# Last part of a two-layer perceiver kernel: attention two tiles ahead of the layers, the first softmax beside the values' products, rounded levels turned before the rounding number is taken off

## The chip, the core and the metric

The kernel runs on one core of one Trainium2 chip. The metric is the device time of one execution in microseconds, here the median of three runs. Engines are named as the profile names them: PE (TensorE, matrix products), PEld (its weight loads), DVE (VectorE), ACT (ScalarE), POOL (GpSimd), SP (SyncE, which issues the DMAs here). PE writes to PSUM, which has eight banks of 512 f32 numbers per partition; the kernel deals them out to pools of two or three buffers.

## The reference, cut to what matters

The whole is six blocks on `x` of 8 batches x 64 queries x 512 numbers (float32), each added to `x`. The first four (a cross attention over 1601 context rows, a spectral block, a routed feed-forward block, a second cross attention) are the same in both kernels. The change touches the last two and the seam before them:

```python
def _L1_attn_ref(x, Wq, Wk, Wv, u, v, Wo, bo):
    # 16 heads of 32
    Q, K, V = heads(x @ Wq), heads(x @ Wk), heads(x @ Wv)
    r = _sinusoid_rel_pos(S, dk)
    term1 = jnp.einsum('bhqd,bhkd->bhqk', Q, K)
    term2 = jnp.einsum('bhqd,kd->bhqk', Q, r)
    term3 = jnp.einsum('hd,bhkd->bhk', u, K)[:, :, None, :]
    term4 = jnp.einsum('hd,kd->hk', v, r)[None, :, None, :]
    scores = (term1 + term3 + _rel_shift(term2 + term4)) / jnp.sqrt(dk)
    attn = jax.nn.softmax(scores, axis=-1)
    out = jnp.einsum('bhqk,bhkd->bqhd', attn, V).reshape(B, S, H * dv)
    return out @ Wo + bo

def _L1_ffn_ref(x, w1, b1, w2, b2):
    def act_quant(x):
        scale = 127.0 / jnp.clip(jnp.max(jnp.abs(x), axis=-1, keepdims=True), 1e-05)
        q = jnp.clip(jnp.round(x * scale), -128.0, 127.0) / scale
        return x + jax.lax.stop_gradient(q - x)
    def bitlinear(x, w, b):
        xq = act_quant(rmsnorm(x))
        wq = weight_quant(w)          # -1, 0 or 1 times one scale
        return jnp.einsum('bsd,fd->bsf', xq, wq) + b
    h = bitlinear(x, w1, b1)          # 512 -> 2048
    h = jax.nn.gelu(h, approximate=False)
    return bitlinear(h, w2, b2)       # 2048 -> 512

x = x + _L1_attn_ref(_layernorm(x, axis=-1), ...)
x = x + _L1_ffn_ref(_layernorm(x, axis=-1), ...)
```

## The kernel before, in words

The 512 query rows are four tiles of 128 rows (two batches of 64 each), kept in SBUF as `x[:, t, :]` throughout. `l1_xattn` is the second cross attention. It goes over eight batches; each makes scores of four head groups against 1601 keys, a softmax, the values' products, and for the batch after it the keys. After batches 2, 4 and 6 begin, `project_out` adds the result to tiles 0, 1 and 2 of `x`; tile 3 is added at the very end. So in the last batch tiles 0 to 2 of `x` are already what the last part reads.

`l1_tail` is the last part: self attention with relative positions, then the two layers. Its steps, by name and line:

- `Group.turn` (L1698 on): normalises a tile (`K.normalizer`, L63; statistics on DVE L81 and L82, the power on POOL L56, the normalised tile `xn` L68), turns it on PE (`xt_ps`, L1702) and copies it on ACT (`xT`, L1703). There is one `xn` buffer. The first group holds tiles 0 to 2, the last group tile 3 alone.
- `Group.queries` (L1712 on): the queries' product (`q_ps`, L1707), from which DVE makes `qu` (L1717) for the scores and ACT makes `qv` (L1725) for the positions. Both read the same PSUM bank, in the order of the code.
- `positions_of` (L1749 on): products of `qv` with the position table (`y_ps`, L1740), copied by DVE and ACT (L49, L51) to `y`, two buffers; four DMAs per tile write `y` to DRAM (`shift`, L1757). `shifted` (L1772 on): four DMAs per tile read it back skewed by one (`z`, L1776), which is the reference's `_rel_shift`.
- `keys_and_values` (L1793 on): keys for a group (`k_ps`, L1707, copied at L1798), then values tile by tile (`v_ps`, L1802).
- `probabilities` (L1808 on): scores (`s_ps`, also L1740, 16 products), `z` added (L1815), then the softmax: maximum L1819, subtraction L1820, exp on ACT L1821, sum L1822, reciprocal L1823, product L1824.
- `turn` (L1827 on), `attend` (L1838 on), `out` (L1861 on): transposes of the probabilities (`pT_ps`, L1833; copies L1834), their product with the values (`o_ps`, L1846), masking to own heads (`oT`, L1855 on ACT and L1856 on DVE), the output product (`out_ps`, L1864) and its addition to `x` (L1871).
- `hidden` (L1873 on): statistics of `x`, normalisation, levels (`rms_levels`, L1614 on), turning (`xT_ps`, L1888, copied at L1889), the first layer in four pieces of 512 (`h_ps`, L1896), scaled by DVE (L1900), GELU (L1901) and squares (L1903) on ACT, maxima on DVE (L1904).
- `hidden_levels` (L1907 on): the levels of all 2048 numbers. `layer2` (L1918 on): turning (`hT_ps`, L1923; copies by `K.copy`, DVE and ACT in turn), the second layer (`o2_ps`, L1927, shown as `o_ps`), scaling with the bias `b2` (L1929), addition of `x` (L1930) and the output DMA (L1931).

`rms_levels` rounds by adding and subtracting 1.5 x 2^23 (`MAGIC`). It makes two passes over its data: one scales in place (L1629), one rounds into a bf16 copy (L1630: `xq`, 512 wide, and `hq`, 2 x 1024).

The order at the end of `l1_tail` is written out by hand:

```python
keys_and_values(first)
p = {0: probabilities(0)}
last.turn(); last.queries(); positions_of(FIRST, last.qv[0])
out(0, attend(0, turn(p[0])))
p[1] = probabilities(1)
keys_and_values(last); shifted(FIRST)
for t in range(NT):
    h = hidden(t)
    if got: layer2(t - 1, *got)
    if t + 1 < NT: out(t + 1, attend(t + 1, turn(p[t + 1])))
    got = hidden_levels(*h)
    if t + 2 < NT: p[t + 2] = probabilities(t + 2)
layer2(NT - 1, *got)
```

(cut, with calls drawn together). This order is not each engine's order word for word. The framework lays out every engine's queue ahead of the run; of what it holds ready it takes what stands first in the code. In the trace PE does some of the last part's L1702 between the cross attention's L1461, and its L1707 keys between L1740 positions. At run time each queue is worked off in its order.

PSUM in the last part: pool `e` three banks (`xt_ps`, `q_ps`, `y_ps`, `h_ps`), pool `mm` three banks (`k_ps`, `v_ps`, `s_ps` two at a time, `pT_ps`, `o_ps` two at a time, `out_ps`, `o2_ps`), pool `t` two (`xT_ps`, `hT_ps`).

Of the kernel before, what the change touches and what calls it, by code (L numbers as in the profile page):

```python
# [10 lines left out]
F32 = mybir.dt.float32  # L11
# [8 lines left out]
P = 128  # L20
# [12 lines left out]
class Ctx:  # L33
# [29 lines left out]
    def normalizer(self, pool, x):  # L63

        _, mv, rstd = self.statistics(pool, x)

        def norm(t, out):
            self.nc.vector.tensor_scalar(  # L68
                out, x[:, t, :], mv[:, t, 0:1], rstd[:, t : t + 1], ALU.subtract, ALU.mult
            )  # L70

        return norm
# [1147 lines left out]
def l1_xattn(K, x, d):  # L1220
# [7 lines left out]
    with ExitStack() as es:  # L1228
# [257 lines left out]
        for b in range(B):  # L1486
# [16 lines left out]

            s[0] = scores(b, 0, r_of[0])
# [47 lines left out]
class TernaryWeights:  # L1552
# [5 lines left out]
    def __init__(self, K, pool, memory, d):  # L1558
        nc = self.nc = K.nc
        self.ident = pool.tile([P, P], BF16, tag="identq", name="identq")  # L1560
        nc.vector.tensor_copy(self.ident, K.ident)
# [52 lines left out]
def rms_levels(K, pool, y, top, mean_square, out):  # L1614
# [10 lines left out]
    nc.vector.tensor_scalar_mul(scale, scale, 127.0)  # L1625
    nc.vector.tensor_scalar_mul(level, top, 1.0 / 127.0)
    n = min(y.shape[-1], 1024)
    for i in range(y.shape[-1] // n):
        nc.vector.tensor_scalar(y[:, ts(i, n)], y[:, ts(i, n)], rms, scale, ALU.mult, ALU.mult)  # L1629
        nc.vector.tensor_scalar(out[:, ts(i, n)], y[:, ts(i, n)], MAGIC, MAGIC, ALU.add, ALU.subtract)  # L1630
# [3 lines left out]
def l1_tail(K, x, d, w):  # L1634
# [8 lines left out]
    with ExitStack() as es:  # L1643
        ep = es.enter_context(tc.tile_pool(name="e_e", bufs=1))
        sp = es.enter_context(tc.tile_pool(name="e_n", bufs=3))
# [41 lines left out]
        class Group:  # L1687
# [8 lines left out]
            def turn(self):  # L1696
                for i, t in enumerate(self.tiles):
                    xn = ep.tile([P, D], F32, tag="xn", name="xn")  # L1698
                    K.normalizer(sp, x[:, t : t + 1, :])(0, xn)
# [11 lines left out]
            def queries(self):  # L1711
                self.qv = [ring("q", "qv") for _ in self.tiles]  # L1712
                for c in range(DC):
                    ps = bank("q_ps")[:, : len(self.tiles) * P]
                    self.project(wq, c, ps)
                    for s in range(2):
                        nc.vector.tensor_scalar(  # L1717
                            self.qu[:, c, :, :, s, :].rearrange("p n b q -> p (n b) q"),
                            ps.rearrange("p (b q) -> p b q", q=S),
                            uv[:, 0, c : c + 1], own[:, s : s + 1], ALU.add, ALU.mult,  # L1720
                        )
                    for i in range(len(self.tiles)):
                        q = ps[:, ts(i, P)].rearrange("p (b q) -> p b q", b=2)
                        for s in range(2):
# [3 lines left out]
                            )  # L1728

# [63 lines left out]
        def keys_and_values(g):  # L1793
            n = len(g.tiles) * P
            for c in range(DC):
                ps = pm.tile([P, D], F32, tag="mm", name="k_ps")[:, :n]
                g.project(wk, c, ps)
                nc.scalar.copy(kT[:, c, ds(g.tiles[0] * P, n)], ps)  # L1798
            for i, t in enumerate(g.tiles):
# [72 lines left out]

        def hidden(t):  # L1873
# [8 lines left out]
            xq = rp.tile([P, D], BF16, tag="xq", name="xq")  # L1882
            level = rms_levels(K, rp, y, top, square, xq)
            nc.vector.tensor_mul(level, level, w.size[:, 0:1])
            xT = rp.tile([P, DC, P], BF16, tag="xT", name="xT")
            ps = pt.tile([P, 4, P], BF16, tag="t", name="xT_ps")
            for c in range(DC):
                nc.tensor.transpose(ps[:, c, :], xq[:, ts(c, P)], w.ident)  # L1888
            nc.scalar.copy(xT, ps)  # L1889
# [3 lines left out]
            for n in range(4):  # L1893
# [10 lines left out]
                nc.vector.tensor_reduce(tops[:, n : n + 1], hn, AX.X, ALU.max, apply_absolute_value=True)  # L1904
            return h, tops, squares

        def hidden_levels(h, tops, squares):  # L1907
# [5 lines left out]
            hq = rp.tile([P, HID], BF16, tag="hq", name="hq")  # L1913
            level = rms_levels(K, rp, h, top, square, hq)
            nc.vector.tensor_mul(level, level, w.size[:, 1:2])
            return hq, level

        def layer2(t, hq, level):  # L1918
            hT = rp.tile([P, 16, P], BF16, tag="hT", name="hT")
            for n in range(4):  # L1920
                ps = pt.tile([P, 4, P], BF16, tag="t", name="hT_ps")
                for i in range(4):
                    nc.tensor.transpose(ps[:, i, :], hq[:, ts(4 * n + i, P)], w.ident)  # L1923
                K.copy(hT[:, ts(n, 4), :], ps)
# [4 lines left out]
            nc.vector.scalar_tensor_tensor(o, ps, level, b2, ALU.mult, ALU.add)  # L1929
            nc.vector.tensor_add(o, o, x[:, t, :])  # L1930
            nc.sync.dma_start(d["out"][ts(t, P), :], o)  # L1931

        keys_and_values(first)
        p = {0: probabilities(0)}
# [5 lines left out]
        out(0, attend(0, turn(p[0])))  # L1940
        p[1] = probabilities(1)
# [128 lines left out]
```

## Time and profile before

| | us |
|---|---|
| median of 3 runs (lowest to highest) | 3293.55 (3289.65 to 3298.74) |
| the profiled execution, whole | 3301.78 |
| the profiled execution, span from first to last instruction | 3300.0 |
| in it: last batch's softmaxes and `xt_ps`, up to the first `q_ps` | 3061 to 3100.5 |
| queries and positions up to the keys' end | 3100.5 to 3141.9 |
| values, first softmax, first output, to `x` of tile 0 | 3141.9 to 3179.4 |
| four layers and three more attentions | 3179.4 to 3300.0 |

Busy time of PE, DVE, ACT and POOL and the mean granted clock of PE in the four rounds of the layers (from `xT_ps` to the next tile's `xT_ps`; the last to the end):

| us | length | PE | DVE | ACT | POOL | clock |
|---|---|---|---|---|---|---|
| 3189.9 to 3213.9 | 24.0 | 12.98 | 18.12 | 10.54 | 1.65 | 0.86 |
| 3213.9 to 3245.1 | 31.2 | 19.42 | 22.80 | 11.84 | 1.65 | 0.83 |
| 3245.1 to 3272.6 | 27.5 | 17.25 | 19.35 | 9.50 | 1.65 | 0.87 |
| 3272.6 to 3300.0 | 27.4 | 17.40 | 13.45 | 7.80 | 0.55 | 0.81 |

A line of a timeline reads: start, length, engine, source line, operation, output<-inputs, shape, xcount, and in brackets the idle time of the engine just before it and what ended that. A line of the chain of waits reads: start, length, engine, what is made, source line, count. A matmul of f32 numbers is two instructions on PE, and counts as two.

### The profile page before, as it was taken

What the parts mean: (1) busy time and instruction counts of PE and PEld (TensorE: products, weight loads), DVE (VectorE), ACT (ScalarE), POOL (GpSimd) and SP (SyncE); (2) the same over time, 40 slices, a digit from 0 to 9 for tenths busy, and PEclk for the clock granted to TensorE, in tenths of its full rate; (3) what the DMA queues carried; (4) which work ended last, traced back from release to release, by engine and by line L of the source; (5) the groups of instructions that cost most, each with busy time, mean ns of one, the idle gap of its engine ahead of it and who ended that gap; (6) DMA issues with size and microseconds to landing.
All of it is one profiled execution on the core that took longest, in us unless ns stands there. A gap on an engine that the chain in (4) does not pass through costs nothing.

```text
span 3300.0 us, 40525 instructions
## 1 busy us (share of the span) xinstructions
PE 3177.1 (96%) x15881; PEld 2158.4 (65%) x15881; DVE 1761.2 (53%) x2946; ACT 845.9 (26%) x1572; POOL 1006.0 (30%) x976
## 2 busy tenths in 40 slices
PE   8999999999999999998899998999999999999976
PEld 6777778888878888885445444556555565555643
DVE  4755556666566656654333235554546445464656
ACT  3232322222233212211012221323233232222233
POOL 5433344443545544420000044224031231312000
PEclk9999999999999999998899999999999999999888
DMA  7255553333455343226288530010100001000330
GB/s 235 75 168 148 173 174 89 96 98 110 122 171 160 103 134 99 88 87 217 84 308 290 185 108 20 22 40 1 41 20 22 31 11 40 11 21 1 100 74 13
DMA packets 314322, 329.03 MB, mean 100 GB/s; under 512 B 35525, under 2 KB 235717, under 8 KB 312981
## 3 DMA queue, kind: packets, MB, share of 16 engines
q1 hardware_dynamic: 310416, 314.88, 30.4%
q10 hardware_dynamic: 3717, 11.57, 0.9%
q8 instruction: 126, 2.06, 0.3%
q14 instruction: 63, 0.52, 0.0%
HBM read 303.30 MB, written 23.10 MB: 99 GB/s over the span
## 4 chain that ended last, share of the span: by engine, by line
PE 89%; DVE 5%; DMA 3%; ACT 1%; issue 1%; POOL 1%; SPq 0%; ACTq 0%; POOLq 0%; DVEq 0%
PE k_ps L1298 11%; PE v_ps L1397 11%; PE x_ps L566 10%; PE x_ps L451 9%; PE z_ps L566 5%; PE s_ps L1411 4%; PE z_ps L451 4%; PE h_ps L1118 3%; PE oe_ps L1145 3%; PE acc L1461 3%; PE y_ps L566 2%; PE y_ps L451 2%; PE sum_ps L1320 2%; PE s_ps L444 1%; PE v_ps L599 1%; PE qk_ps L237 1%
## 5 line engine op out<-in xcount | busy, mean ns | idle before, releaser
L1335 POOL TENSOR_TENSOR r<-r,minus_half 128x24 f32<-128x24 f32 x64 | 288.8, 4516 | 747.3 <-DVE r L1331 747.3
L1397 PE MATMUL v_ps<-L1x_WvT,ctxT 128*128 128x512 f32 (+1 forms) x832 | 379.7, 604 | 0.0
L1298 PE MATMUL k_ps<-ctxT,L1x_WkT 128*128 128x384 f32 (+1 forms) x1024 | 375.0, 509 | 0.6 <-ACT o L51 0.6
L451 PE MATMUL x_ps<-qt,ctxT 128*128 128x256 f32 x1152 | 287.2, 383 | 7.6 <-DVE s L416 6.0
L566 PE MATMUL x_ps<-pt,ctx 128*128 128x256 f32 x1152 | 280.3, 381 | 1.4 <-ACT u L514 0.9
L1298 PEld LDWEIGHTS k_ps<-ctxT,L1x_WkT 128*128 128x128 f32 x1024 | 184.0, 189 | 140.2 <-issue 42.8
L1397 PEld LDWEIGHTS v_ps<-L1x_WvT,ctxT 128*128 128x128 f32 (+1 forms) x832 | 149.6, 187 | 170.9 <-issue 164.8
L451 PEld LDWEIGHTS x_ps<-qt,ctxT 128*128 128x128 f32 x1152 | 217.4, 191 | 49.2 <-DVE s L416 10.1
L566 PEld LDWEIGHTS x_ps<-pt,ctx 128*128 128x128 f32 x1152 | 216.5, 189 | 35.1 <-DVE a L541 1.6
L122 POOL TENSOR_TENSOR ctxT<-ctxT 128x256 f32<-128x256 f32 x96 | 79.7, 831 | 402.6 <-DMA ctxT<-in_ctxT 355.2
L1411 PEld LDWEIGHTS s_ps<-qb,kT 64*128 64x128 f32 x1664 | 143.8, 187 | 74.8 <-DVE s L1423 44.1
L432 DVE TENSOR_TENSOR m<-m,s 128x512 f32<-128x512 f32 x176 | 134.5, 764 | 94.2 <-ACT s L430 91.6
L122 POOL TENSOR_TENSOR ctx<-ctx 128x256 f32<-128x256 f32 x96 | 72.4, 754 | 344.6 <-DMA ctx<-in_ctx 279.3
L1411 PE MATMUL s_ps<-qb,kT 64*128 64x128 f32 x1664 | 170.9, 287 | 6.7 <-DVE s L1423 6.3
L1302 ACT ACTIVATE kT<-k_ps,L1x_bk 128x384 f32<-128x384 f32 (+1 forms) x128 | 76.1, 594 | 348.9 <-PE k_ps L1298 343.6
L1331 DVE TENSOR_SCALAR r<-sumT_ps 128x12 f32<-128x12 f32 (+1 forms) x128 | 16.5, 166 | 254.5 <-PE sumT_ps L1328 254.1
L1400 ACT COPY v<-v_ps 128x512 f32<-128x512 f32 (+1 forms) x104 | 60.7, 583 | 335.1 <-PE v_ps L1397 335.1
L1423 DVE TENSOR_TENSOR s<-s_ps,r 128x512 f32<-128x512 f32 x192 | 124.7, 683 | 33.3 <-PE s_ps L1411 33.1
L484 DVE TENSOR_TENSOR s<-s,top_ps 128x1024 f32<-128x1024 f32 (+1 forms) x112 | 123.3, 1137 | 21.3 <-PE top_ps L474 21.3
L1452 DVE TENSOR_TENSOR s<-s,top_ps 128x1664 f32<-128x1664 f32 x64 | 117.9, 1884 | 30.0 <-PE top_ps L1448 30.0
L1431 DVE TENSOR_TENSOR fold<-s 128x1536 f32<-128x1536 f32 x64 | 112.1, 1752 | 37.3 <-ACT s L1453 37.3
L416 DVE SCALAR_TENSOR_TENSOR s<-y_ps,bias,p 128x256 f32<-128x256 f32 x96 | 46.3, 483 | 142.9 <-PE y_ps L451 138.4
(408 smaller groups left out, 5777.6 us busy)
## 6 DMA issues: line engine op xcount, KB each, us to landing
w<-in_L0f_W SPq DMA_DIRECT2D x64, 1024.0 KB, 5.5
ctxT<-in_ctxT SPq DMA_DIRECT2D x192, 256.0 KB, 4.5
ctx<-in_ctx SPq DMA_DIRECT2D x192, 256.0 KB, 3.2
ctxT<-in_ctxT SPq DMA_DIRECT2D x24, 768.0 KB, 4.4
wvT<-in_L0x_WvT SPq DMA_DIRECT2D x16, 1024.0 KB, 6.9
qk<-qk_all SPq DMA_DIRECT2D x15, 1024.0 KB, 6.9
qk_all<-stage SPq DMA_DIRECT2D x32, 384.0 KB, 3.4
wraw<-in_L1f_w1T SPq DMA_DIRECT2D x16, 512.0 KB, 4.2
```

The lines of the kernel that those rows point to most:

```text
L122: nc.gpsimd.tensor_add(q[:, 4, :], q[:, 2, :], q[:, 3, :])
L432: nc.vector.tensor_max(self.m, self.m if k else self.s[:, LAST, :], self.s[:, k, :])
L451: nc.tensor.matmul(ps, lhsT=ctxT[i][:, Quarters.LEFT[n], ts(e, P)], rhs=right[n][:, e, :], start=start and e == 0, stop=e == 1, skip_group ...
L484: nc.vector.tensor_sub(s[:, k : k + n], s[:, k : k + n], top.unsqueeze(1).to_broadcast([P, n, HALF]))
L566: nc.tensor.matmul(ps, lhsT=ctx[pair][:, Quarters.LEFT[n], ts(m, P)], rhs=right[n][:, i, :], start=start and i == 0, stop=i == 2, skip_gro ...
L1298: nc.tensor.matmul(ps[:, :n], lhsT=wk[:, e, ts(c, P)], rhs=ctxT[i][:, e, :n], start=e == 0, stop=e == DC - 1)
L1335: nc.gpsimd.tensor_tensor(r[:, at : at + n, :], r[:, at : at + n, :], minus_half[:, :n, :], ALU.pow)
L1397: nc.tensor.matmul(ps[:kn], lhsT=ctxT[i][:, c, ds(at, kn)], rhs=wv[:, c, :], start=c == 0, stop=c == DC - 1)
L1411: nc.tensor.matmul(pair[j][:, i, :], lhsT=kT[c][rows, ts(k0 + i, P)], rhs=qb[rows, c, b].rearrange("p h q -> p (h q)"), start=True, stop=True,
L1423: nc.vector.tensor_mul(out, in_, by)
L1431: nc.vector.tensor_tensor(t, s[:, :, 0:6, :], s[:, :, 6:12, :], op)
L1452: nc.vector.tensor_sub(s[:, j], s[:, j], ps[:, j, :].unsqueeze(1).to_broadcast([P, NK, P]))
```

## The change

It does five things.

1. The statistics of tiles 0 to 2 are made in a pool of their own before the last batch's scores in `l1_xattn` (a callback `in_last`), and handed to the first group's normaliser as `known`.
2. In `queries`, ACT's `qv` stands ahead of DVE's `qu`.
3. `keys_and_values` is two functions. The order is now: first group's keys, probabilities of tile 0, first group's values, output of tile 0, probabilities of tile 1, the last group's turning, queries and positions, output of tile 1, the last group's keys and values. In the loop over the layers, the probabilities and the output are those of tile t + 2.
4. `rms_levels` makes one pass: scale and `MAGIC` added, in place, in f32. The turning on PE is of these f32 numbers (with the f32 identity; the bf16 one is gone), and `MAGIC` comes off in the copy out of PSUM (`turn_levels`): on ACT for `xT`, on DVE and ACT in turn for the four pieces of `hT`. The buffers `xq` and `hq` are gone.
5. `b2` is added to `x` on POOL at the end of `hidden`, and `layer2`'s two DVE operations become one.

```diff
-    def normalizer(self, pool, x):
-        _, mv, rstd = self.statistics(pool, x)
+    def normalizer(self, pool, x, known=None):
+        _, mv, rstd = known or self.statistics(pool, x)
...
+            if not more:
+                in_last()
             s[0] = scores(b, 0, r_of[0])
...
-def rms_levels(K, pool, y, top, mean_square, out):
+def rms_levels(K, pool, y, top, mean_square):
...
     nc.vector.reciprocal(scale, top)
-    nc.vector.tensor_scalar_mul(scale, scale, 127.0)
-    nc.vector.tensor_scalar_mul(level, top, 1.0 / 127.0)
+    nc.vector.tensor_scalar(scale, scale, 127.0, rms, ALU.mult, ALU.mult)
     n = min(y.shape[-1], 1024)
     for i in range(y.shape[-1] // n):
-        nc.vector.tensor_scalar(y[:, ts(i, n)], y[:, ts(i, n)], rms, scale, ALU.mult, ALU.mult)
-        nc.vector.tensor_scalar(out[:, ts(i, n)], y[:, ts(i, n)], MAGIC, MAGIC, ALU.add, ALU.subtract)
+        nc.vector.tensor_scalar(y[:, ts(i, n)], y[:, ts(i, n)], scale, MAGIC, ALU.mult, ALU.add)
+    nc.vector.tensor_scalar_mul(level, top, 1.0 / 127.0)
     return level
...
-                    K.normalizer(sp, x[:, t : t + 1, :])(0, xn)
+                    K.normalizer(rp, x[:, t : t + 1, :], known[t] if t < FIRST else None)(0, xn)
...
+        def turn_levels(y, out, by_vector):
+            ps = pt.tile([P, 4, P], F32, tag="t", name="levels_ps")
+            for i in range(4):
+                nc.tensor.transpose(ps[:, i, :], y[:, ts(i, P)], K.ident)
+            if by_vector:
+                nc.vector.tensor_scalar_add(out, ps, -MAGIC)
+            else:
+                nc.scalar.activation(out, ps, AF.Identity, bias=w.down, scale=1.0)
...
+            nc.gpsimd.tensor_add(x[:, t, :], x[:, t, :], b2)
             return h, tops, squares
...
             for n in range(4):
-                ps = pt.tile([P, 4, P], BF16, tag="t", name="hT_ps")
-                for i in range(4):
-                    nc.tensor.transpose(ps[:, i, :], hq[:, ts(4 * n + i, P)], w.ident)
-                K.copy(hT[:, ts(n, 4), :], ps)
+                turn_levels(h[:, ts(n, 512)], hT[:, ts(n, 4), :], n % 2 == 0)
...
-            nc.vector.scalar_tensor_tensor(o, ps, level, b2, ALU.mult, ALU.add)
-            nc.vector.tensor_add(o, o, x[:, t, :])
+            nc.vector.scalar_tensor_tensor(o, ps, level, x[:, t, :], ALU.mult, ALU.add)
             nc.sync.dma_start(d["out"][ts(t, P), :], o)
...
-        keys_and_values(first)
-        p = {0: probabilities(0)}
+        keys(first)
+        p = probabilities(0)
+        values(first)
+        out(0, attend(0, turn(p)))
+        p = probabilities(1)
         last = Group(wp, [FIRST])
         last.turn()
         last.queries()
         positions_of(FIRST, last.qv[0])
         groups.append(last)
-        out(0, attend(0, turn(p[0])))
-        p[1] = probabilities(1)
-        keys_and_values(last)
+        out(1, attend(1, turn(p)))
+        keys(last)
+        values(last)
         shifted(FIRST)
         got = None
         for t in range(NT):
             h = hidden(t)
             if got:
                 layer2(t - 1, *got)
-            if t + 1 < NT:
-                out(t + 1, attend(t + 1, turn(p[t + 1])))
+            if t + 2 < NT:
+                p = probabilities(t + 2)
             got = hidden_levels(*h)
             if t + 2 < NT:
-                p[t + 2] = probabilities(t + 2)
+                out(t + 2, attend(t + 2, turn(p)))
         layer2(NT - 1, *got)
...
+        known = []
+        with tc.tile_pool(name="early", bufs=NT - 1) as sp:
+            l1_xattn(K, x, d, lambda: known.extend(K.statistics(sp, x[:, t : t + 1, :]) for t in range(NT - 1)))
+            l1_tail(K, x, d, w, known)
```

## The prediction

> **What bounds the kernel now.** The page first: PE is busy for 96% of the span, but the granted clock and PE's digits fall off in the last slices, and the whole change lies there, from about 3061 us on. So the next view is the chain of waits. Its last lines (start, length, engine, what, line):
>
> ```profile
> 3173.31 5.27 PE out_ps L1864 x8
> 3191.02 3.64 PE h_ps L1896 x16
> 3199.29 5.40 PE out_ps L1864 x8
> 3215.21 3.88 PE h_ps L1896 x12
> 3230.49 5.40 PE out_ps L1864 x8
> 3246.40 3.64 PE h_ps L1896 x12
> 3261.45 5.41 PE out_ps L1864 x8
> 3273.91 5.23 PE h_ps L1896 x12
> 3290.93 4.12 PE o_ps L1927 x15
> ```
>
> The chain passes four times from the attention's output product (L1864) to the first layer's product (L1896): the layers of tile t+1 wait for its attention, and that attention (its ACT copies and oT among them) waits behind tile t's GELUs. A round takes 31.2 us (from 3199.29 to 3230.49). PE is no bound inside it, and no other engine is, as busy times by stretch show (columns as its first line names them, clock and DMA share behind):
>
> ```profile
> core 0: us, PE busy (x) PEld busy (x) DVE busy (x) ACT busy (x) POOL busy (x), PEclk, DMA share, GB/s
> 3152.00:3179.40 27.40, 21.60 (x165) 16.32 (x165) 11.74 (x20) 7.36 (x15) 0.00 (x0) 0.75 0.55 147
> 3179.40:3300.00 120.60, 75.68 (x476) 40.44 (x474) 83.28 (x186) 42.40 (x85) 6.61 (x12) 0.86 0.03 9
> 3205.00:3214.00 9.00, 1.70 (x31) 1.56 (x30) 8.00 (x20) 1.06 (x1) 1.10 (x2) 0.81 0.00 1
> 3228.00:3236.00 8.00, 5.51 (x12) 2.22 (x12) 2.48 (x6) 2.08 (x3) 0.00 (x0) 0.79 0.09 35
> 3272.60:3300.00 27.40, 17.40 (x84) 8.21 (x84) 13.45 (x29) 7.80 (x17) 0.55 (x1) 0.81 0.05 20
> ```
>
> DVE is busiest with 83.28 of 120.60. Where a softmax and a layer's start share it, it runs 8.00 of 9.00; where all wait for the output product, 2.48 of 8.00. That hole is what the change can fill. Last, the timeline of the lead-in:
>
> ```profile
> 3086.88 0.30 PE L1702 MATMUL xt_ps<-ident,xn 128*128 128x128 f32 x1 [2.72 <-DVE xn L68]
> 3093.13 0.69 PE L1461 MATMUL acc<-s,v 128*64 128x128 f32 x2 [2.17 <-ACT s L1453]
> 3111.83 6.40 ACT L1725 ACTIVATE qv<-q_ps,vs,c_own 128x128 f32<-128x128 f32 x18 [4.89 <-DVE qu L1717]
> 3121.64 18.83 SPq L1757 DMA_DIRECT2D shift<-y  x12
> 3140.51 9.89 SPq L1776 DMA_DIRECT2D z<-shift  x12
> 3158.15 1.28 DVE L1815 TENSOR_TENSOR p<-s_ps,z 128x512 f32<-128x512 f32 x2
> 3167.24 1.97 PE L1833 MATMUL pT_ps<-ident,p 128*128 128x128 f32 x8 [1.95 <-DVE p L1824]
> 3178.69 0.69 DVE L1871 TENSOR_TENSOR x<-x,out_ps 128x512 f32<-128x512 f32 x1 [5.43 <-PE out_ps L1864]
> ```
>
> Scores of tile 0 stand behind the values' products on PE (24 of them, 10.46 us), though z has been under way since 3140.51; and qv, which everything behind z hangs on, waited 4.89 us for DVE's qu.
>
> **Step 1, statistics early and qv first.** Three tiles' statistics (0.69 + 0.18 + 0.15 us each on DVE, 3.1 us, and three powers of 0.55 on POOL) go before the last batch's scores. I cost them at nothing: DVE stands idle there for 7.04 and 6.14 us at a time behind sumT_ps, and nothing reads them before 3067; without this cover they cost 3.1 us of that batch's DVE chain. They then no longer hold xn, so the turns (L1702) and the first q_ps can go into PE's waits of 2.17, 0.49 and 0.31 us: q_ps ends 3.0 us before today's 3114.5 (bounds 0 and 5.9, the sum with the 2.72 and 0.19 us waits). With qv ahead of qu the last column's six (0.37 us apart, 2.2) end 2.2 us behind q_ps, 3113.7 instead of 3118.2: y, shift and z come 4.5 us earlier (bounds 0 and 6). qu comes later by those 2.2 us; only scores read it, 25 us later. y has two buffers, so the third still waits for the first one's shift on SP; that moves along.
>
> **Step 2, scores and softmax of tile 0 ahead of the values.** z of tile 0 is four of the twelve reads: issued from 3136.0, the fourth 2.5 us later, landing 4.9 us (the median) on, 3143.4. Keys end at 3141.9 - 3.0, scores (2.00) at 3140.9, so DVE's first add waits for z and starts at 3143.4, not 3158.15. Behind it on DVE stand only copies of v; on PE, two of the three mm banks are held until the add, so the second v_ps waits about 1 us. Softmax: 1.28 + 1.21 + 1.22 + 1.06 + 1.22 + 0.25 + 1.22 with 0.3 of handover is 7.7, and a copy of v between, 0.7: done at 3151.8. Values end at 3140.9 + 10.5 + 1 = 3152.4; now the transposes wait for PE, not PE for p. From there 1.04 (eight transposes, as at 3221.08), 0.7 copy, 1.10 o_ps, 1.4 oT, the output product, 0.75 add. That product is 3.6 us by L1476 (clock full) and 5.4 by L1864 (clock lowered after idling); I take 4.5, since PE has now been busy before it. Sum 9.5: x of tile 0 is ready at 3162 instead of 3179.4, **-17.4** (-13 without step 1, -21 with all of it and 3.6).
> The last tile's group moves behind that attention; its products (q 4.04, y 4.2 us on PE) fill PE's waits under the second softmax, and its four shift and four z transfers on SP move later with nothing behind them but the first output at 3229. Tile 3's softmax, which needs them, comes some 40 us later. Cost 0; if it fell behind x of tile 0, DVE's part is 3.6 us.
>
> **Step 3, the loop.** What stays after 3162 is the same work as after 3179.4 now, with these edits. Out: xq 0.43, hq 2 x 0.65, the last add 0.69, times four: 9.6 us of DVE. In: two of four hT copies on DVE from f32 (0.69, as L49 for y) instead of bf16 (0.42), times four: 2.2. DVE: 83.3 - 9.6 + 2.2 = 75.8. On ACT three copies per tile grow from 0.59 to about 0.70 (an estimate from L1302: 0.594 with a bias for 384 columns, 128 more). On PE 80 transposes go from about 0.08 to 0.13 us, 4 us in all, of which a fifth on the path. The add of b2 goes to POOL at 1.27 (L1806), busy 6.61 of 120.6; behind it stands the power of the hidden levels (0.55), due some 8 us later; without that cover 5.1 us.
> The last tile's layers run alone, now 27.4 us: the first half of h is ready 1.35 us sooner (one pass, not two), the last add is gone (0.7), the f32 turning adds 0.9: 26.3, with 11.9 of DVE. The other 63.9 us of DVE now come from two tiles that don't wait for each other: the layers of t+1 find x ready, softmax and output of t+2 fill in. At what share does DVE run? Between today's 0.73 (22.80 of 31.2 in the third round) and 1; the row of 8.00 in 9.00 is two chains sharing it without the hole; I take 0.85, since banks in the mm pool are handed out in turn (tile 1's scores wait for tile 0's output product, layer 2 waits for out of t+2). 63.9 / 0.85 = 75.2; with 26.3, 101.5 instead of 120.6: **-19.1** (-6.8 at 0.73, -30.4 at 1).
>
> Exp beside GELU: five table loads of 1.283 us lie in this stretch now; if the exp of tiles 2 and 3 falls between GELUs, four more, 5.1 us on ACT, which is busy 42.4 of 120.6; I take 0 on the path, 5.1 as its end. The Trainium skill, ScalarE: Activation LUTs, section "Table sets: the hidden batching unit", speaks against this change: one set's functions should be done in a batch, and its section "What ACT_TABLE_LOAD costs" charges about 2.66 us a switch with the drain. By that the four would be 10.6 us (an estimate from the page) and the gain 26 instead of 36; the row has half the price and is used.
>
> **Sum.** -17.4 - 19.1 = -36.5 us. The profiled execution took 3301.78 us, 3300.0 of it span; that is 8 us over the median of the runs, 3293.55, to which I apply the difference: **3257 us**.
>
> **Rivals.** *DVE becomes the bound*: share 1 in the loop, -17.4 - 30.4 = -48, **3246**. For it: DVE is the busiest engine already. Against it: waits for POOL's powers (0.73 us each) and for exp have to be filled every time.
> *The loop keeps its rhythm*: the mm banks and the DVE queue hold layers t+1 behind out of t+2, so only cheaper work and the lead count: -13 - 6.8 = -20, **3274**. For it: scores of tile 1 came at 3178.51, right behind L1864, although PE had idled at 3160; banks in turn do that. Against it: the first product h_ps has banks of its own.
> *Slower, the code's order carried out without overlap*: softmax and output of t+2 stand in DVE's and PE's queues between the layers of t and t+1, and in-order engines wait in them. From 3162: four layers of 23.9 (27.4 without its last 3.5), 3.5, three softmaxes of 8.4 and three outputs of 9.5 make 152.8, ending at 3314.8: +14.8, **3308**. It decides from 138 us on (3300 - 3162). For it: one wait in order at the wrong place costs a round. Against it: the same pieces share DVE today at 8.00 of 9.00.
> *It doesn't do what it says*: z lands no sooner than today's add, and step 2 is worth nothing but clock; then -36.5 + 14 = -22, inside the second rival's place.
>
> **How the numbers follow.** Forecast 0.58, DVE-bound 0.15, rhythm kept (with z late) 0.21, slower 0.06. The range leaves out the slower case, half of what lies lowest (0.07) and the weakest of the second rival (0.04): 3241 to 3280. About 0.3% (9.9 us) can be told from no change by this measurement; all of the forecast and the first rival and most of the second are beyond it: faster 0.90, same 0.04, slower 0.06.
>
> **What would show it.** Right: the first L1815 near 3143 with v_ps beside it; no idle time of PE between L1443 and q_ps over 1 us; x of tile 0 near 3162; h_ps of tile 1 beginning less than 25 us behind h_ps of tile 0; DVE above 0.8 until the last tile's h_ps near 3237. Wrong: the first add still behind v_ps, rounds of 30 us, exp between GELUs with nine table loads, or DVE waiting for banks.

## The result, and the profile after

The changed kernel took 3286.61 us (median of 16 runs, 3281.98 to 3291.04) against 3294.07 us (16 runs, 3288.59 to 3300.45) of the kernel before run beside it: a ratio of 0.9977, 95% interval 0.9969 to 0.9986. On another chip it was 0.9970 (0.9959 to 0.9981). It is faster by 7.5 us, not by the 36.5 of the forecast, and lies outside the range.

The profiled execution took 3286.85 us, 3285.1 of it span. Both kernels do the same work up to the last part, but end it at different times from one execution to the next, so times from here on are counted from the issue of the Wq read (L1671 now, L1673 before), at 3066.92 in the profile before and 3070.08 in the one after. The "last part" runs from there to the end of the span; its "lead" ends with L1871 of tile 0, when x of that tile is ready.

| us | before | after |
|---|---|---|
| first z read issued (L1776 / L1774) | 73.6 | 61.0 |
| first addition of z (L1815) | 91.2 | 77.5 |
| lead: x of tile 0 ready | 112.5 | 97.3 |
| first layer of tile 0 under way (L1896 / L1902) | 124.1 | 126.1 |
| last part | 233.1 | 215.0 |
| from x of tile 0 to the end | 120.6 | 117.7 |

So the lead became 15.2 us shorter, the layers of tile 0 began 2 us later, and everything from x of tile 0 on took 2.9 us less, where the forecast had 19.1. The chain of waits of the kernel after:

```profile
3161.42 5.21 PE out_ps L1864 x8
...
3173.79 5.37 PE y_ps L1738 x32
...
3185.91 3.43 PE out_ps L1864 x8
3189.35 3.57 PE k_ps L1705 x32
3192.92 3.44 PE v_ps L1802 x8
3196.35 3.24 PE h_ps L1902 x15
...
3218.90 3.55 PE out_ps L1864 x8
```

Before, it went from the output product of tile 0 (3173.31) straight to h_ps (3191.02). Now the last group's positions (y_ps), the output of tile 1 and the last group's keys and values stand between: 28.8 us from x of tile 0 (3167.4) to the layers (3196.2). Busy times by stretch of the kernel after (columns as before: length, PE, PEld, DVE, ACT, POOL, then clock, DMA share, GB/s):

```profile
3167.40:3196.19 28.79, 24.80 (x155) 18.91 (x154) 16.25 (x37) 6.09 (x13) 4.16 (x5) 0.76 0.21 37
3196.19:3262.14 65.95, 43.88 (x289) 25.95 (x287) 50.58 (x118) 31.76 (x59) 6.85 (x10) 0.85 0.02 7
3262.14:3285.10 22.96, 16.17 (x77) 8.82 (x76) 11.99 (x25) 7.39 (x16) 0.55 (x1) 0.87 0.08 28
3167.40:3285.10 117.70, 84.85 (x518) 53.68 (x516) 78.82 (x180) 45.24 (x88) 11.56 (x16) 0.84 0.08 19
```

DVE is busy for 78.82 of 117.70, a share of 0.67; before it was 83.28 of 120.60, 0.69. Without the layers of the last tile, which run alone, it is 66.83 of 94.74, 0.71 (before: 69.83 of 93.20, 0.75): 0.77 between the first layers of tiles 0 and 3, 0.56 ahead of them. Next, DVE's timeline in the lead, and two lines of PE's:

```profile
3138.13 0.69 DVE L49 COPY v<-v_ps 128x512 f32<-128x512 f32 x1 [13.79 <-PE v_ps L1802]
3146.99 0.69 DVE L49 COPY v<-v_ps 128x512 f32<-128x512 f32 x1 [8.17 <-PE v_ps L1802]
3147.60 1.28 DVE L1815 TENSOR_TENSOR p<-s_ps,z 128x512 f32<-128x512 f32 x2
...
3166.73 0.69 DVE L1871 TENSOR_TENSOR x<-x,out_ps 128x512 f32<-128x512 f32 x1 [5.37 <-PE out_ps L1864]
...
3179.99 0.54 DVE L1890 TENSOR_SCALAR y<-x,lt_mv,lt_rstd 128x512 f32<-128x512 f32 x1
```

```profile
3155.33 1.97 PE L1833 MATMUL pT_ps<-ident,p 128*128 128x128 f32 x8 [6.60 <-DVE p L1824]
...
3212.00 1.11 PE L1877 MATMUL levels_ps<-ident,y 128*128 128x128 f32 x4 [10.47 <-DVE y L1628]
```

Two copies of the values stand ahead of the first addition of z in DVE's queue, and the second waits 8.17 us for PE. The softmax is behind the values' products, not beside them, and PE then idles 6.60 us for it. The normalisation of tile 0 for the layers (L1890) comes 12.6 us after x of that tile, behind the second softmax. In the loop PE waits 10.47 us at one place for DVE: the engines take turns instead of working side by side.

### The profile page after: what moved, and what is told of

The parts are those of the page before. It is cut to its first block, busy times and chain, and to the rows that moved or that the text cites. A ratio compares the mean times of both kernels' runs of the same rounds, so it can differ in the third digit from the quotient of the medians.

```text
span 3285.1 us, 40503 instructions
## 1 busy us (share of the span) xinstructions
PE 3174.3 (97%) x15881; PEld 2162.1 (66%) x15881; DVE 1749.7 (53%) x2929; ACT 846.4 (26%) x1572; POOL 1008.8 (31%) x980
## 4 chain that ended last, share of the span: by engine, by line
PE 89%; DVE 4%; DMA 3%; ACT 1%; issue 1%; POOL 1%; ACTq 0%; SPq 0%; POOLq 0%; DVEq 0%
PE k_ps L1298 11%; PE v_ps L1397 11%; PE x_ps L566 10%; PE x_ps L451 9%; PE z_ps L566 5%; PE s_ps L1411 4%; PE z_ps L451 4%; PE h_ps L1118 3%; PE oe_ps L1145 3%; PE acc L1461 3%; PE y_ps L566 2%; PE y_ps L451 2%; PE sum_ps L1320 2%; PE s_ps L444 1%; DMA w_out<-wq 1%; PE v_ps L599 1%
## 5 line engine op out<-in xcount | busy, mean ns | idle before, releaser
L484 DVE TENSOR_TENSOR s<-s,top_ps 128x1024 f32<-128x1024 f32 (+1 forms) x112 | 123.3, 1137 | 20.7 <-PE top_ps L474 20.7
```

Source lines behind the costliest of these rows:

```text
L484: nc.vector.tensor_sub(s[:, k : k + n], s[:, k : k + n], top.unsqueeze(1).to_broadcast([P, n, HALF]))
```

## The experiments

Each kernel is the changed one with the edit shown, unless "before" is named. Times in us from the issue of the Wq read; "clock" is the mean granted clock of the first 66 us; ratios are to the kernel before on the same chip, with 95% intervals.

| run | clock | z issued | lead | x of tile 0 to end | last part | ratio |
|---|---|---|---|---|---|---|
| before (two profiles) | 0.81, 0.90 | 73.6, 67.5 | 112.5, 107.8 | 120.6, 122.0 | 233.1, 229.8 | 1 |
| after (three profiles) | 0.95 | 61.1 | 97.3 to 97.9 | 117.6 to 117.7 | 215.0 to 215.7 | 0.9977, 0.9970 |
| e_order_alone | 0.92 | 67.6 | 104.7 | 124.2 | 228.9 | 1.0003 (0.9990 to 1.0016) |
| e_rounding_alone | 0.90 | 68.5 | 104.2 | 117.6 | 221.8 | 0.9983 (0.9971 to 0.9994) |
| e_head_alone | 0.95 | 61.1 | 98.0 | 120.4 | 218.4 | 0.9967 (0.9954 to 0.9979) |
| e_head_again | 0.92 | 62.4 | 100.9 | 121.8 | 222.7 | 0.9980 (0.9967 to 0.9992) |
| e_old_order | 0.95 | 61.1 | 99.4 | 115.7 | 215.1 | 0.9975 (0.9962 to 0.9988) |
| e_v_on_act | 0.95 | 61.1 | 91.5 | 116.5 | 208.1 | 0.9945 (0.9927 to 0.9964) |
| e_v_again | 0.87 | 65.2 | 98.5 | 117.8 | 216.3 | 0.9956 (0.9939 to 0.9972) |
| e_last_kv_later | 0.87 | 65.2 | 101.9 | 123.3 | 225.2 | 0.9976 (0.9960 to 0.9992) |
| e_last_q_sooner | 0.87 | 65.2 | 103.9 | 111.5 | 215.4 | 0.9965 (0.9948 to 0.9983) |
| e_q_and_hidden | 0.95 | 61.1 | 99.5 | 121.5 | 221.0 | 0.9992 (0.9977 to 1.0006) |
| e_p_before_hidden | 0.95 | 61.1 | 94.3 | 123.6 | 217.9 | 0.9959 (0.9945 to 0.9973) |
| e_out_before_layer2 | 0.95 | 61.1 | 94.0 | 120.6 | 214.6 | 0.9960 (0.9947 to 0.9974) |
| e_identq_kept | 0.95 | 61.1 | 98.2 | 117.7 | 215.9 | 0.9961 (0.9946 to 0.9975) |
| e_identq_again | 0.87 | 65.2 | 101.9 | 121.5 | 223.4 | 0.9968 (0.9953 to 0.9982) |
| e_identq_v | 0.87 | 65.3 | 95.7 | 116.5 | 212.2 | 0.9949 (0.9930 to 0.9967) |

**How far one profile carries.** Before and after, unchanged, were profiled again.

> The kernel before, unchanged, for a second profile: in the first one the last part, from the issue of the Wq read to the end of the span, took 233.1 us, but that execution lay 8 us above the median. Theory A (the head, which both kernels share, varies from execution to execution by several us and the last part does not): the last part is again 231 to 235 us, and whatever the total differs by lies ahead of the Wq read. Rival B (the last part itself varies): the last part is some 225 us, 8 less than in the first profile.

> The changed kernel, unchanged, for a second profile: in the first one the last part, from the issue of the Wq read to the end, took 215.05 us. Theory A (the last part is steady, the head varies): 213 to 217 us again, with the Wq read issued anywhere between 3062 and 3074. Rival B (the last part varies, and the first profile caught a short one): 220 us or more.

The changed kernel's last part repeated (215.3), the one before's was 3.3 us shorter (229.8), of which its lead gave 4.7: the profile that the prediction started from had a clock of 0.81 in the first 66 us, the second 0.90. So neither A nor B held outright.

**The values' copies.**

```diff
-                K.copy(v[:, t, :], ps)
+                nc.scalar.copy(v[:, t, :], ps)
```

> The changed kernel with every copy of the values on ACT instead of DVE and ACT in turn. Theory: the first softmax fell behind the values' products because DVE's queue holds two copies of v ahead of the addition of z, so that DVE waited 8.17 us for v_ps. Then the first addition (L1815) comes within 1.5 us of z's landing, some 8 us sooner than in the changed kernel (counted from the issue of the Wq read: 69.5 instead of 77.55 us), and x of tile 0 is final 5 to 8 us sooner. The end comes at most 3 us sooner, since the first product of the layers still stands behind the last group's products on PE. Rival 1: the lead is what sets the end, and the whole gain of 5 to 8 us arrives there. Rival 2: the addition does not move because z lands no sooner than v_ps ends.

The first addition came at 69.0 instead of 77.5, x of tile 0 5.8 us sooner, and the end 6.9 us sooner: the first rival, not the theory. In the table the stretch from x of tile 0 to the end stays where it was (116.5 against 117.7), so whatever shortens the lead arrives. DVE's and ACT's timelines of this run:

```profile
3138.07 1.29 DVE L1815 TENSOR_TENSOR p<-s_ps,z 128x512 f32<-128x512 f32 x2 [14.13 <-DMA z<-shift]
...
3147.49 1.22 DVE L1822 TENSOR_REDUCE m<-p 128x16 f32<-128x1024 f32 x1 [5.62 <-ACT p L1821]
```

```profile
3145.92 0.58 ACT L1805 COPY v<-v_ps 128x512 f32<-128x512 f32 x1 [3.79 <-PE v_ps L1802]
3146.40 1.06 ACT L1821 ACTIVATE p<-p 128x1024 f32<-128x1024 f32 x1
```

Now the addition waits for z and nothing else, but the exp waits in ACT's queue behind the copies (4.5 us from 3141.9, when its input was done). The wait has changed its queue, and is shorter there.

**The last group's keys and values.** Moved behind the layers' start of tile 0:

```diff
-        keys(last); values(last); shifted(FIRST)
...
             h = hidden(t)
+            if t == 0:
+                keys(last); values(last); shifted(FIRST)
```

> The changed kernel with the last group's keys, values and shifted reads moved behind the layers' start of tile 0 in the order of the code. Theory: the last tile's keys and values (3189.2 to 3196.2 in the profile) stand ahead of h_ps of tile 0 on PE, though its input is turned at 3185.5; then the first h_ps begins some 7 us sooner (119 instead of 126 us from the issue of the Wq read) and the end comes 3 to 7 us sooner. Rival: DVE sets the pace from x of tile 0 on, so h_ps starts sooner but the end moves by less than 2 us either way. A loss would say that tile 3's softmax then waits for its keys.

The rival: the layers began at 123.6, the rounds behind the first took 31 us again, and the ratio stayed at the changed kernel's (0.9976). At the same clock of 0.87 the changed kernel (e_identq_again, below, which adds a copy that nothing reads) had its layers under way at 132.3 and ended at 223.4, against 225.2 here: starting them 8.7 us sooner did not bring the end forward.

**Which part did it.** The old order with everything else of the change; the new order alone on the kernel before; and the two other parts alone on it (statistics and qv first: "head"; one-pass rounding, f32 turning, b2 on POOL: "rounding").

For e_old_order, with calls drawn together (e_order_alone makes the same exchange the other way in the kernel before; the head and rounding runs take over their hunks of the diff above unchanged):

```diff
-        keys(first); p = probabilities(0); values(first); out(0, attend(0, turn(p))); p = probabilities(1)
+        keys(first); values(first); p = {0: probabilities(0)}
         last = Group(wp, [FIRST]); last.turn(); last.queries(); positions_of(FIRST, last.qv[0])
-        out(1, attend(1, turn(p)))
+        out(0, attend(0, turn(p[0]))); p[1] = probabilities(1)
         keys(last); values(last); shifted(FIRST)
...
-            if t + 2 < NT:
-                p = probabilities(t + 2)
+            if t + 1 < NT:
+                out(t + 1, attend(t + 1, turn(p[t + 1])))
             got = hidden_levels(*h)
             if t + 2 < NT:
-                out(t + 2, attend(t + 2, turn(p)))
+                p[t + 2] = probabilities(t + 2)
```

> The changed kernel with the order of the last part as it was before (values before the first softmax, last group before the first output, attention one tile ahead); statistics, qv first, the rounding and b2 on POOL stay. Times from the issue of the Wq read, of which the end comes at 230 to 233 us before and at 215 after. Theory: the order shortened the loop by interleaving h_ps with the attention of t+2 on PE, and paid it back by putting the last group's products and a softmax ahead of h_ps of tile 0. Then here z is issued at 61, x of tile 0 is final near 102, h_ps of tile 0 starts near 114 (126 in the changed kernel), and the rounds are again some 28 us (PE's queue has all 16 h_ps together), so the end comes at 214 to 220: the order as a whole was worth 5 us or less. Rival: the order carries the whole gain of 15 to 18 us; the end comes at 227 or later.

> The kernel before with only the new order of the last part (statistics, qu first, rounding in two passes and b2 as before). Theory: z is issued at 67.5 as in the kernel before, the first addition waits for the values' copies (some 10 us behind z's issue), h_ps of tile 0 starts near 131, and the loop behind it takes 93 to 97 us (88.9 after, 109 to 110 before; the two-pass rounding costs back some 6): end at 224 to 230 us, a gain of at most 6. Rival 1: the order alone makes the loop 89 us, end at 220. Rival 2: without the cheaper rounding the interleave is lost, the loop stays at 109, and the end comes at 240, a loss of 8 us.

> The kernel before with only the statistics made early and qv ahead of qu. Theory (two parts that add up: this one and the rounding make the 15 to 18 us of the last part by themselves, the order nothing): z is issued at 61 instead of 67.5 to 73.6 us from the issue of the Wq read, x of tile 0 final near 101, the end at 220 to 225 instead of 230 to 233; the median some 4 us lower than before. Rival: the sooner z is waited away behind the values and DVE in the loop; the end stays at 228 or later.

> The kernel before with the early statistics and qv ahead of qu alone, again. Theory: these two give what the whole change gives: the median within 3 us of the changed kernel's on this chip, the last part 217 to 220 us at the full clock. Rival: the rounding adds to them, and the changed kernel is 4 us or more below this one.

> The kernel before with only the rounding in one pass, the f32 turning and b2 on POOL. Theory: z at 67.5 as before, h_ps of tile 0 at 119 to 121, and the loop from there 105 us as in the run with the old order instead of 110, so the end comes at 224 to 227; the median some 4 us lower than before. Rival: the 7.5 us of DVE work taken out of the loop lie off its chain (DVE is busy for 0.65 of it) and the end moves by under 2 us.

The old order ends at 215.1, as the new one does; alone, the new order changes nothing that can be measured (1.0003), so the theory held in both runs. The head parts alone bring the lead from 107.8 to 98.0, nearly all of what the change gains there, and leave the rest as it was (120.4). The rounding takes 3 to 5 us out of the rest (117.6 against 120.6 and 122.0; with the head parts on both sides 115.7 against 120.4). In its own run the lead, which it doesn't touch, was shorter too, so the end there says less. Taken one by one the two parts promise a ratio of 0.995 to 0.996 (0.9967 or 0.9980 times 0.9983), more than the whole change gives (0.9977 and 0.9970); why they don't add up, no run shows. The rounding leaves DVE's share about where it was:

```profile
3168.20:3283.90 115.70, 76.99 (x469) 45.12 (x474) 76.37 (x170) 43.31 (x85) 13.35 (x16) 0.85 0.03 10
```

(e_old_order, from x of tile 0: DVE 76.37 of 115.70, 0.66.) What the order does can be read off against this run: the layers of tile 0 start at 126.1 instead of 109.8, and the time from there is 88.9 instead of 105.3. Sixteen us were moved from one side of that mark to the other. Counted from x of tile 0, the new order even makes the rest 2 to 4 us longer (117.7 against 115.7; 124.2 against 120.6 and 122.0), and the lead 2 to 3 us shorter (97.3 against 99.4; 104.7 against 107.8). The first addition of z, which it was to bring forward, comes at 74.8 in e_old_order and at 77.5 in the changed kernel.

**Can the early start be had too?** Four more orders, all with the values' copies on ACT: the last group's queries ahead of tile 0's output; also the layers of tile 0 ahead of the second softmax; and two in which the attention of t + 2 stands further forward in the loop.

The first, e_last_q_sooner, and the second, e_q_and_hidden, which has both of these:

```diff
+        last = Group(wp, [FIRST]); last.turn(); last.queries(); positions_of(FIRST, last.qv[0])
         out(0, attend(0, turn(p)))
```

```diff
+        h = hidden(0)
         p = probabilities(1)
```

The loops of e_p_before_hidden and of e_out_before_layer2:

```diff
+            p = probabilities(t + 2)
             h = hidden(t)
+            out(t + 2, attend(t + 2, turn(p)))
             layer2(t - 1, *got)
```

```diff
             h = hidden(t)
+            p = probabilities(t + 2)
+            out(t + 2, attend(t + 2, turn(p)))
             layer2(t - 1, *got)
```

> The changed kernel with the values' copies on ACT (end at 208.1 us from the issue of the Wq read) and the last group's turning, queries and positions ahead of tile 0's output in the code. Theory: its 8 us of PE work and 3.6 us of DVE work lie in the waits of the first output instead of between x of tile 0 and h_ps of tile 0, so h_ps of tile 0 starts at 112 to 116 instead of 120.3, x of tile 0 comes up to 3 us later than 91.5, the loop keeps its interleave (87.8 us from the first h_ps), and the end comes at 201 to 205. Rival: PE is in the way of tile 0's transposes, x of tile 0 comes 6 us later and the end stays at 207 to 210.

> As the run with the last group's queries sooner, and with the layers' start of tile 0 ahead of the second softmax in the code. Theory: h_ps of tile 0 starts about 12 us behind x of tile 0, at 104 to 108 us from the issue of the Wq read, but PE's queue then has no interleave in the loop (16 h_ps together, the attention of t+2 behind them), so the rounds are 29 to 31 us as in the run with the last group's keys later, and the end comes at 205 to 215: starting the layers 15 us sooner is worth nothing. Rival: the loop takes 88 us wherever it starts, and the end comes at 192 to 196.

> The changed kernel with the values' copies on ACT (end at 208.1 us from the issue of the Wq read), and in the loop the probabilities of t+2 ahead of the layers' start of t and its output ahead of the second layer of t-1. Theory: the place of the attention in PE's queue sets the loop, not its length of look-ahead: here tile 3's attention is done a round sooner, the last two rounds hold layers alone, and the end comes at 200 to 206. Rival: the softmax of tile 2 now stands ahead of tile 0's h on DVE, and the first round loses what the last ones gain: 207 to 213.

> The changed kernel with the values' copies on ACT, and in the loop both the probabilities and the output of t+2 ahead of the second layer of t-1 and behind the layers' start of t. Theory: PE keeps h_ps of tile 1 interleaved with tile 2's attention (rounds of 20 and 24 us as with the copies alone) and tile 3's attention moves ahead of the second layer of tile 1, so the end comes at 202 to 207 against 208.1. Rival: the second layer of tile t-1, now later, holds h's buffer and the next layers: 208 to 214.

The second is the plainest. PE's timeline of e_q_and_hidden:

```profile
3175.22 1.89 PE L1902 MATMUL h_ps<-w1q,xT 128*128 128x512 bf16 x4 [0.78 <-ACT xT L1881]
...
3204.20 3.40 PE L1902 MATMUL h_ps<-w1q,xT 128*128 128x512 bf16 x15 [0.57 <-ACT xT L1881]
...
3220.02 5.09 PE L1864 MATMUL out_ps<-L1a_Wo,oT 128*128 128x512 f32 x8 [1.47 <-DVE oT L1856]
...
3233.84 4.72 PE L1902 MATMUL h_ps<-w1q,xT 128*128 128x512 bf16 x15 [0.74 <-ACT xT L1881]
...
3263.71 5.31 PE L1902 MATMUL h_ps<-w1q,xT 128*128 128x512 bf16 x16 [0.34 <-ACT xT L1881]
```

The layers begin 18 us sooner than in the changed kernel (at 108.5), every round then takes 29 to 30 us, with all of h_ps ahead of the attention of t + 2, and the end is 6 us later, 13 later than with the copies alone. The two loops with the attention further forward end behind their rivals' figures as well (217.9 and 214.6), each with one round of 28 to 29 us. The first one met the low clock, so e_v_again with the same 0.87 is what to hold it against: the lead grew by 5.4 us (98.5 to 103.9), the rest shrank by 6.3 (117.8 to 111.5), since work of the last group now lay ahead of x of tile 0, and the end came 0.9 sooner, which is its rival. Its ratio (0.9965) is no better than that of the copies alone (0.9945 and 0.9956).

**The removed identity.** The last part was 15 to 18 us shorter in the profiles, the median 7.5. Did the change make the head later, through the bf16 identity it removes? It was put back, unread, in the changed kernel and in e_v_on_act.

> The changed kernel, unchanged, timed beside the three others on one chip. Theory: ratio to before 0.997 to 0.998 again; the last part 215 us where the granted clock is 1.00 in the 30 us behind the Wq read, and some 4 us more where it is 0.9 there.

> The changed kernel with the values' copies on ACT, again. Theory: the last part 208 us at the same clock, 5 to 7 us below the changed kernel's median on this chip, ratio to before 0.9945 to 0.996. Rival: the first result was one of few executions on a chip that suited it, and the difference to the changed kernel is under 3 us.

> The changed kernel with the removed bf16 identity and its copy put back (nothing reads it), so that the head has the instructions and the addresses of before. Theory A (the head's end scatters by itself): the Wq read is issued anywhere in 3060 to 3070, as in all runs so far, and the median is that of the changed kernel, run beside it, within 3 us. Rival B (the change makes the head later): the Wq read is issued at 3063 or before and the median is 3 to 5 us below the changed kernel's.

> The changed kernel with the removed bf16 identity and its copy put back, again. Theory A (the head's end scatters by itself, and the first result was chance): ratio to before 0.997 to 0.998 as for the changed kernel (0.9977 and 0.9970). Rival B (without the identity the head ends later): 0.996 again or lower, and the Wq read issued at 3064 us or before.

> The same with the values' copies on ACT. Theory A: ratio to before 0.9945 to 0.9956, as without the identity. Rival B: 3 to 5 us lower still, 0.993 to 0.9945. Under both the last part takes 208 us at the full clock and some 216 at the lower one seen in the second run of the copies on ACT.

The runs don't settle it. The first came out as rival B had it: the Wq read at 3061.1, the median (3281.39) 6.6 us under that of the changed kernel on the same chip (3288.02). The second lies near theory A: 0.9968, against 0.9977 and 0.9970 for the changed kernel, with overlapping intervals, and the Wq read at 3064.0. With the copies on ACT the identity makes no difference (0.9949 beside 0.9945 and 0.9956). The head's end scatters by itself: two profiles of one kernel (e_head_alone, e_head_again) issue the Wq read at 3061.4 and 3070.5. But over all 20 profiles it is issued at 3063.9 on average in the eight with the identity (3060.5 to 3070.5) and at 3067.0 in the twelve without (3060.4 to 3071.2). From the first to the 31st maximum of the second cross attention (L1445) pass 1016.5 to 1016.9 us in all eight, and 1016.8 to 1017.2 in nine of the twelve, but 1020.1 to 1020.2 in the other three. A head some 3 us later without the identity fits this, and isn't shown.

The copies on ACT have the lowest ratios in three comparisons of 5 or 6 runs each, 6.0 us under the changed kernel on the one chip where both ran (3282.05 against 3288.02). The intervals of those two ratios overlap; that it is no chance is said by the last part, which is shorter at either clock (208.1 against 215.0 to 215.7 at 0.95; 216.3 and 212.2 against 223.4 at 0.87).

## Why the prediction was wrong

**Step 1 was right, in size too.** The statistics cost nothing that shows: from the first to the 31st maximum of the second cross attention pass 1016.8 and 1016.9 us in the two profiles before, 1016.6 and 1016.5 with the head parts alone. Between the first two profiles the first y_ps moved by 6.2 us (47.5 to 41.3), but their clocks differ; at the same clock of 0.92 it comes 4.8 us sooner (48.9 in e_order_alone, 44.2 in e_head_again) and z is issued 5.2 us sooner (67.6 and 62.4). The text had 4.5. (Its bounds of 0 and 6 don't follow from its terms: 0 to 5.9 from PE's waits and 1.5 from the order of qv and qu make 1.5 to 7.4.) With the head parts alone taking 7 to 11 us off the last part (222.7 and 218.4 against 229.8) and reaching the changed kernel's ratios (0.9967 and 0.9980 beside 0.9977 and 0.9970), this step is the bulk of the gain.

**Step 2 got its time for another reason.** It put the first addition 76.5 us behind the Wq read (3143.4 in its profile), waiting for z, and x of tile 0 at 95.1; measured 77.5 and 97.3. But z had landed by 69.0, as e_v_on_act shows. The sentence "Behind it on DVE stand only copies of v" is where it failed: two of them stand ahead, and DVE, which took them in order, waited 8.17 us for products that PE had not yet made. With this wait the new order is worth 0.7 to 3.1 us of the lead (97.3 against 98.0 with the head parts alone; the pairs above), and 5.8 more come with the copies out of DVE's queue. The lead looks nearly as forecast (15.2 us shorter, where the text had 17.4) because step 1 and the baseline filled in: the profile that the text started from had a clock of 0.81 there, and the second one, at 0.90, a lead 4.7 us shorter.

**"Cost 0" for the last group was wrong.** Its products didn't fill waits under the second softmax. The second softmax, its queries, the output of tile 1 and its keys and values took their turns between x of tile 0 and its layers: 28.8 us, against 11.6 before, with 5.37 of positions (y_ps) on the chain itself. Taking the queries and positions out of that stretch (e_last_q_sooner) made the rest 6.3 us shorter, where the text's own end for this term was 3.6.

**Step 3 is the term that failed.** It divided 63.9 us of DVE work by a share of 0.85, added 26.3 for the last tile, and came to 101.5 from x of tile 0; 117.7 was measured. The work was right (75.8, and 3.6 for the last group, against 78.82 measured), and so, nearly, was the last tile (22.96 from its h_ps). The share was not: ahead of the last tile's layers it was 0.71, where the same stretch had 0.75 before; over all of it, it lies between 0.63 and 0.69 in every one of the 20 profiles. The text took a row of 9 us in which two chains happened to overlap as the rule for 75 us. Of the 19.1 us, the cheaper rounding gave 3 to 5, and the order none: it made the stretch 2 to 4 us longer, and the end stayed where it was in the pairs that differ by it alone (229.8 against 228.9, at clocks of 0.90 and 0.92; 215.1 against 215.0). Rounds did become shorter (from 24.2, 31.2 and 27.5 us to 19.5, 24.5 and 22.0), which the list of signs would have counted as a success ("h_ps of tile 1 beginning less than 25 us behind", which the kernel before met as well): the attention of tile 1 had only been moved out of them. In any of the seven orders run, with the copies on ACT or without, the profiles show 116 to 124 us from x of tile 0 to the end, but for the one that did part of the work before. That the chains wait for each other in queues worked off in order is how the waits read (PE's 10.47 us for DVE, DVE's 8.17 for PE); no run took the queues out of it.

**Rivals.** "The loop keeps its rhythm" came nearest (3274 against 3286.61), by its sum rather than its picture. What b2 on POOL costs or saves no run tests by itself. The exp between GELUs cost nothing: five table loads before and after, and five even in e_q_and_hidden, where the exp of tile 2 does lie between two GELUs. The text's four more were a misreading: the five of before hold the switches to exp for tiles 2 and 3 and back already. The Trainium skill (ScalarE: Activation LUTs, "What ACT_TABLE_LOAD costs") has 2.66 us a switch with the drain; in that run ACT goes from the load at 3207.74 through exp (1.06) and a second load to the next GELU at 3211.40, so 1.3 us a switch, and the measurement decides.

**What stays open.** Profiles of the last part differ by 14.1 to 18.1 us between the kernels, medians by 7.5 and 8.5. All three profiles of the changed kernel met the clock of 0.95; at 0.87, with the identity back, its last part was 223.4, only 6.4 us below the 229.8 of the kernel before at 0.90. Together with the scatter of the head (9 us in one kernel) and a head that may end some 3 us later without the identity, this is large enough to make up the difference, but that it does was not shown.

## What to carry to other kernels

A shorter round proves nothing if work has left the loop on the other side: measure from a mark that all orders share to the end, and run the order alone and everything but the order. Before a chain is counted as lying beside another, list what stands ahead of its first instruction in each in-order queue, and for how long the products those wait for will keep PE. An overlap share read from one short stretch was here an upper end (0.89 in 9 us), not a value (0.71 over 95 us).

## What the runs showed of the hardware

One instruction stream runs its first 66 us at different granted clocks. The stretch of 5 us that begins 20 us behind the Wq read, and all 66, of e_identq_kept and of e_identq_again, the same kernel:

```profile
3081.10:3086.10 5.00, 3.92 (x21) 2.45 (x20) 4.42 (x4) 2.73 (x3) 0.00 (x0) 1.00 0.00 2
3061.10:3127.10 66.00, 63.23 (x504) 45.43 (x503) 38.98 (x58) 20.93 (x39) 0.98 (x5) 0.95 0.49 93
```

```profile
3084.00:3089.00 5.00, 3.92 (x17) 2.42 (x16) 4.04 (x4) 2.08 (x3) 0.00 (x0) 0.59 0.01 2
3064.00:3130.00 66.00, 63.23 (x467) 45.50 (x466) 39.06 (x58) 20.46 (x38) 0.98 (x5) 0.87 0.37 87
```

PE is busy equally long in both, but the clock of the 5 us is 1.00 in one and 0.59 in the other, that of the 66 us 0.95 and 0.87, and z is issued 4.1 us later. The second execution's last part is 7.5 us longer in all (223.4 against 215.9). These two ran on different chips; but e_v_again, with 0.87, shared its chip with after_timed and e_identq_kept, with 0.95. The Trainium skill (TensorE: Matmul & The Clock Gate, "What's actually happening") says that the window over which PE's activity is judged runs freely of the kernel, which fits; the window itself is not seen in these traces. One profile of each kernel thus can't tell a gain of 8 us in this part.
